# Graph kernel on one core: columns of h and of scores laid out by partition group

## Chip, cores and metric

The kernel runs on one core of a Trainium2 chip. The metric is device time in microseconds for one execution of the whole program, as a median of several runs. Smaller is better.

## What is computed

x holds 64 graphs of 256 nodes with 512 features each, in float32; adj is one 256 x 256 adjacency matrix of zeros and ones, shared by all graphs. Two residual layers follow each other:

```python
# layer 0
h = maximum(layernorm(x), 0)
q, k, v = h @ Wq.T, h @ Wk.T, h @ Wv.T
rel = adj.T * (q @ k.T)                     # per graph, 256 x 256
rel = rel / norm(rel, axis=-1)
x = x + rel @ v
# layer 1
h = maximum(layernorm(x), 0)
x = x + (adj @ h) @ weight + bias
```

## The kernel before

**Precision.** Each float32 operand of a large product is split into three parts of fewer bits, with the suffixes u, l and s. A product is three passes of matmuls; before the third, ScalarE scales the bank in place (L340). So one product of 512 x 512 by 512 rows costs 12 matmuls of 512 columns, and each operand needs one pass of ScalarE and two of VectorE for its parts (L238 to L249, L316 to L318, L471 to L473).

**Tiling.** The graphs are taken in 32 pairs of two (512 rows, as four chunks of 128 rows on the partitions). M = Wq.T Wk is formed once. For each pair there are six stages: g (`g_stage`, gy = M times h transposed, from m_u, m_l, m_s and h_u, h_l, hs), v (`v_stage`), the scores (`scores`), the weighted sum (`attend`), layer 1's sum over neighbours (`gather`) and its product with weight (`mix`). `gather` and `mix` of a pair run during the next pair. A pair begins on TensorE with the first matmul bank<-h_u,m_u, and that is how pairs are told apart here; they are numbered from 0.

**Order.** `Plan` takes operations with an engine, a cost, keys that they read and write, a time to landing and, for some, a number of microseconds by which they should be early. `order` gives each a due time, counted back from an ideal TensorE, and then simulates the engines to choose an order. That order is written out by hand to each engine: every engine runs strictly in it. An instruction that waits holds all that stand behind it on its engine.

**Two transposes by way of VectorE.** Products need h, and later the scores, with features or neighbours on the partitions. VectorE transposes 32 x 32 blocks only (`V.transpose`). So the 16 combinations of four partition groups of 32 and four column groups of 32 are first exchanged: 16 DMAs within SBUF carry the block (k, j) to partition group j, column group k.

- h: the relus (L279, one for each of the four chunks) write h_rel, which is `[chunk c, 512 features]`; `h_place` (L293) copies it into blocks, and `h_turn` (L301) transposes blocks into ht. `h_parts` splits ht into h_u (L316, ScalarE), h_l (L318) and hs (L308). In h_rel the 32 columns of one group are 128 bytes, so each DMA takes 512 pieces of 128 bytes.
- scores: `scores` multiplies the bank with adj transposed and writes rel, which is the first half of h_rel (L415, VectorE), and squares it for the norm (L419, ScalarE). `turn_scores` copies rel into placed, the second half of h_rel, by 16 DMAs of 256 pieces of 128 bytes (L455), and transposes placed into raw (L461), from which rel_u, rel_l and rel_s_parts come (L471, L472, L473). For pairs 0, 1 and 31, TensorE transposes the scores instead (L437).

h_rel thus serves twice in a pair: the scores of pair i, then h of pair i + 1.

**SP's queue.** SP issues, in its fixed order, the 16 placements of h of the next pair, the load of x for the pair after that into fresh (L257), the load of x for the running pair into x_ring, and the 16 placements of scores. The statistics of fresh (L265, L266 on VectorE) wait for that load. Stores of finished pairs go out from POOL's queue (L564).

Of the kernel before, what the change touches and what calls it, by code (L numbers as in the profile page):

```python
# [12 lines left out]
AF = mybir.ActivationFunctionType  # L13
# [95 lines left out]
def f(ap):  # L109
    return ap.bitcast(F32)  # L110
# [3 lines left out]
def kernel(  # L114
# [11 lines left out]
    nc = tc.nc  # L126
    P = 128
    B, N, D = x.shape
    DC = D // P
    NC = N // P  # L130
    NB = 2
    TC = NB * NC
    T = NB * N
    NP = B // NB
    S = 32
# [18 lines left out]
    ht, h_s = [None, None], [None, None]  # L154
# [5 lines left out]
    blocks = room("blocks", TC, DC, P)  # L160
    h_rel = room("h_rel", TC, D)
    bias_bc = room("bias_bc", D)
    wv_sb, w_sb = blocks.rearrange("p c d n -> p c (d n)"), ring[1]
    ident = room("ident", P)
# [16 lines left out]
    def raw():  # L181
        return changing("rel_s", "raw", NB, D)

    def rel_third():
        return changing("rel_s", "parts", NB, NC, NC, P, dtype=F32R)

    flat_rel = h_rel.rearrange("p c d -> p (c d)")
    rel = flat_rel[:, : T * NC].rearrange("p (b k m) -> p b k m", b=NB, k=NC)
    placed = flat_rel[:, T * NC :].rearrange("p (b k t n) -> p b k t n", b=NB, k=NC, t=NC)

    stats = [
        [
# [15 lines left out]
    V, A, G, SP = nc.vector, nc.scalar, nc.gpsimd, nc.sync  # L208
# [10 lines left out]
        (in_pieces.add if turned else in_pieces.discard)(n)  # L219
        return bank[n], ("bank", n)  # L220

    placed_all = [("blocks", j, k) for j in range(P // S) for k in range(P // S)]

    def keys(name, n=DC):
        return [(name, k) for k in range(n)]
# [56 lines left out]
    def h_rows(plan, i, src=fresh, name="fresh"):  # L282
        relu, needs = norm(plan, i, 0, src, name)
        for c in range(TC):
            plan.add("ACT", 0.72, lambda c=c: relu(h_rel[:, c, :], c),
                     [(name, c), *needs], [("h_rel", c)])

    def h_place(plan, early=8.0):
        hv = h_rel.rearrange("p c (d e) -> p c d e", e=P)

        for j in range(P // S):
            for k in range(P // S):
                plan.add("SP", 0.65, lambda j=j, k=k: SP.dma_start(  # L293
                    out=blocks[ts(j, S), :, :, ts(k, S)], in_=hv[ts(k, S), :, :, ts(j, S)]),
                    keys("h_rel", TC), [("blocks", j, k)], lands=2.3, early=early)

    def h_turn(plan):
        def turn(k):
            ht[k] = room(f"ht{k}", 2, T, tag=f"h_s{k}")
            for d in range(2):  # L300
                V.transpose(ht[k][:, d].rearrange("p (c n) -> p c n", c=TC), blocks[:, :, 2 * k + d])  # L301
        for k in range(2):
            plan.add("DVE", 1.16, lambda k=k: turn(k), placed_all, [("h_s", 2 * k), ("h_s", 2 * k + 1)])

# [99 lines left out]
    def scores(plan, i):  # L404
        rn = norms[i % 2]
        for b in range(NB):
            def outs_of(ps, k, d, b=b):
                return [
                    (ps[:, ts(n, N)], gy[k][:, d, ts(b * NC + n, P)], hp(k, d)[:, ts(b, N)])
                    for n in range(NC)  # L410
                ]
            first, second = three(None, None, gy_half(b), h_named, 2 * HALF, outs_of)

            def drain(ps, key, b=b):
                plan.add("DVE", 0.6, lambda: V.tensor_mul(  # L415
                    rel[:, b].rearrange("p k m -> p (k m)"), ps, f(adjt[0]).rearrange("p k m -> p (k m)")),
                    [key, "adjt"], [("h_rel", b)])
                for k in range(NC):
                    plan.add("ACT", 0.53, lambda k=k: A.activation(  # L419
                        ps[:, ts(k, N)], rel[:, b, k], AF.Square, accum_out=rn[:, b, k : k + 1]),  # L420
                        [("h_rel", b)], [key, (f"rn{i % 2}", b, k)])
            unit(plan, first, second, drain)

    def turn_scores(plan, i, by_pe=False):
        rn, name = norms[i % 2], f"rn{i % 2}"
        sums = [(name, b, k) for b in range(NB) for k in range(NC)]
        plan.add("ACT", 0.2, lambda: A.activation(rn, rn, AF.Sqrt), [], sums)
        plan.add("DVE", 0.12, lambda: V.reciprocal(rn, rn), [], sums)
        if by_pe:
            u, l = (part.rearrange("p b t k n -> p b (t k n)") for part in rel_p)  # L430
            for b in range(NB):
                ps, key = next_bank(turned=True)

                def go(ps=ps, b=b):
                    for t in range(NC):
                        for k in range(NC):
                            nc.tensor.transpose(ps[:, ts(t * NC + k, P)], rel[:, b, k, ts(t, P)], ident)  # L437

                def third(b=b):
                    V.scalar_tensor_tensor(rel_third()[:, b].rearrange("p t k n -> p (t k n)"),  # L440
                                           f(l[:, b]), CROSS, f(u[:, b]), op0=ALU.mult, op1=ALU.subtract)
                plan.add("PE", 0.44, go, [("h_rel", b)], [key])
                plan.add("ACT", 0.49, lambda ps=ps, b=b: A.activation(
                    u[:, b], ps, AF.Copy, scale=NEAR), [key], [("rel_u", b)])
                plan.add("DVE", 0.63, lambda ps=ps, b=b: V.tensor_sub(
                    l[:, b], ps, f(u[:, b])), [key, ("rel_u", b)], [("rel_l", b)])
                plan.add("DVE", 0.6, third, [("rel_u", b), ("rel_l", b)],
                         [("raw", 0), ("raw", 1)] if not b else [("raw", 1)])
            return
        rv = rel.rearrange("p b k (t m) -> p (b k t) m", m=P)  # L450
        pv = placed.rearrange("p b k t n -> p (b k t) n")

        for j in range(P // S):
            for k in range(P // S):
                plan.add("SP", 0.65, lambda j=j, k=k: SP.dma_start(  # L455
                    out=pv[ts(j, S), :, ts(k, S)], in_=rv[ts(k, S), :, ts(j, S)]),
                    [("h_rel", 0), ("h_rel", 1)], [("placed", j, k)], lands=2.1)
        halves, rel_u, rel_l = ([(name, b) for b in range(NB)] for name in ("raw", "rel_u", "rel_l"))
        for b in range(NB):
            for k in range(NC):  # L460
                plan.add("DVE", 0.33, lambda b=b, k=k: V.transpose(  # L461
                    raw()[:, b].rearrange("p (t k n) -> p t k n", t=NC, k=NC)[:, :, k], placed[:, b, k]),
                    [("placed", j, t) for j in range(P // S) for t in range(P // S)] + [("h_rel", 2), ("h_rel", 3)], halves if not b and not k else halves[b : b + 1])

        def whole(ap):
            return ap.rearrange("p b t k n -> p (b t k n)")

        def flat_raw():
            return raw().rearrange("p b d -> p (b d)")
        u, l = (whole(part) for part in rel_p)  # L470
        plan.add("ACT", 0.96, lambda: A.activation(u, flat_raw(), AF.Copy, scale=NEAR), halves, rel_u)  # L471
        plan.add("DVE", 1.14, lambda: V.tensor_sub(l, flat_raw(), f(u)), [*halves, *rel_u], rel_l)  # L472
        plan.add("DVE", 1.14, lambda: V.scalar_tensor_tensor(  # L473
            whole(rel_third()), f(l), CROSS, f(u), op0=ALU.mult, op1=ALU.subtract), [*rel_u, *rel_l], halves)
# [204 lines left out]
    def pairs(exact):  # L679
# [15 lines left out]
        v_stage(plan, 0, exact, (0, 1))  # L695
        scores(plan, 0)
        v_stage(plan, 0, exact, (2, 3))
        turn_scores(plan, 0, by_pe=True)
        finish(plan)
        h_turn(plan)  # L700
        h_parts(plan)
# [3 lines left out]
        for i in range(1, NP):  # L705
            last = i + 1 == NP
            load(plan, i, name=f"x{i % 2}")
            if not last:
                h_rows(plan, i + 1)
                h_place(plan)  # L710
            if i + 2 < NP:
                load(plan, i + 2)
            g_stage(plan, i)
            v_stage(plan, i, exact, (0,))
            v_stage(plan, i, exact, (1,), hold=True)
            scores(plan, i)
            gather(plan, i - 1, exact)
            while held:
                held.pop(0)()
            if last or i == 1:  # L720
                turn_scores(plan, i, by_pe=True)
            v_stage(plan, i, exact, (2, 3))
            if not last:
                if i > 1:
                    turn_scores(plan, i)
                waiting.append(lambda: (h_turn(plan), h_parts(plan)))
                mix(plan, i - 1)
            attend(plan, i, exact)
            if last:
                mix(plan, i - 1)  # L730
                gather(plan, i, exact)
            store(plan, i - 1)
# [37 lines left out]
```

## Time and profile before

| | before |
|---|---|
| runs | 1570.98, 1572.20, 1574.19 us; median 1572.2 |
| profiled execution | 1571.74 us, span 1570.0 us |
| instructions in the profile | 22385 |
| placements of h | 496 DMAs of 64 KB, 2.1 us from issue to landing |
| placements of scores | 464 DMAs of 32 KB, 1.9 us |
| loads into fresh | 31 DMAs of 1 MB, 5.9 us |
| loads into x_ring | 31 DMAs of 1 MB, 7.9 us |
| transposes of h, L301 | 124 of 128x512, 688 ns each |
| transposes of scores, L461 | 116 of 128x256, 404 ns each |
| products with adj, L415 | 64 of 128x512, 691 ns each |
| relus into h_rel, L279 | 124 of 128x512, 808 ns each |
| squares, L419 | 128 of 128x256, 391 ns each |

The profile records one execution; its own time is beside its span. Engine names are PE (TensorE matmul), PEld (its weight loads), DVE (VectorE), ACT (ScalarE), POOL, and SPq for SP's issues of DMAs. Matmuls overlap, and their ends are modelled, so the length of a matmul in the profile is more than the distance from one to the next; where PE loses time is seen in the distance of starts. A wait is written as waiter <- releaser. Times in windows are counted from the start of the span.

### The profile page before, as it was taken

Reading aid. Unit: us, or ns where it says so; the run is one execution under the profiler, and the core shown is the slowest. Engines: PE = TensorE matmul, PEld = TensorE weight load, DVE = VectorE, ACT = ScalarE, POOL = GpSimd, SP = SyncE. Lnnn points to the kernel's source line nnn. Section 1 sums busy time; section 2 is a strip of 40 time slices with the busy share of each in tenths; the row PEclk is TensorE's granted clock in tenths of the full one; section 3 lists DMA queues with packets and bytes.
Section 4 is the critical chain, followed back from the end, with each engine's and each line's share of the span. In section 5 each row is a group of like instructions: output and inputs, shape, how many; then the busy total and the mean of one; then the engine's idle time right before and its main releaser. Section 6 shows DMA issues by size and latency. Waiting matters only on the chain.

```text
span 1570.0 us, 22385 instructions
## 1 busy us (share of the span) xinstructions
PE 1557.2 (99%) x8046; PEld 1322.8 (84%) x8046; DVE 1357.6 (86%) x2419; ACT 1023.8 (65%) x1941; POOL 24.3 (2%) x39
## 2 busy tenths in 40 slices
PE   9999999999999999999999999999999999999998
PEld 6788888888888888888888888888888888888886
DVE  6997889898888988898888889888989888988786
ACT  5567666676667676666666676766666766767654
POOL 0000000000000000000000000000000000000000
PEclk9999999999999999999999999999999999999999
DMA  6431444324444334443244442344433344433311
GB/s 195 113 81 41 118 111 120 69 77 111 115 115 93 82 81 120 110 119 68 77 112 114 114 112 67 81 118 111 118 75 85 97 119 110 121 67 79 84 54 56
DMA packets 433127, 153.62 MB, mean 98 GB/s; under 512 B 389872, under 2 KB 390128, under 8 KB 433008
## 3 DMA queue, kind: packets, MB, share of 16 engines
q1 hardware_dynamic: 422784, 116.46, 31.5%
q0 software_dynamic: 8432, 32.51, 5.6%
q10 hardware_dynamic: 1792, 3.15, 0.5%
q8 instruction: 65, 1.06, 0.3%
q14 instruction: 54, 0.44, 0.1%
HBM read 70.78 MB, written 33.55 MB: 66 GB/s over the span
## 4 chain that ended last, share of the span: by engine, by line
PE 83%; SPq 5%; DVE 5%; DMA 4%; ACT 2%; issue 1%; ACTq 0%; DVEq 0%
PE bank L228 83%; SPq L293 4%; DMA fresh<-in_x_dram 2%; SPq L455 2%; ACT h_rel L279 1%; DVE st L265 1%; DMA bias_bc<-in_L_gnn_bias_dram 1%; DMA x_ring<-in_x_dram 1%; DMA h_rel<-h_rel 0%; DVE gy_s L239 0%; DVE gy_l L241 0%; ACT bank L340 0%; DVE h_rel L415 0%; DVE late_parts L239 0%; DVE mv L266 0%
## 5 line engine op out<-in xcount | busy, mean ns | idle before, releaser
L340 ACT ACTIVATE bank<-bank 128x512 f32<-128x512 f32 x572 | 333.4, 583 | 321.5 <-PE bank L228 318.3
L228 PE MATMUL bank<-wv_s,hs 128*128 128x512 f32 x512 | 139.9, 395 | 0.2
L228 PE MATMUL bank<-w_u,gy_u 128*128 128x512 f32 x512 | 137.9, 391 | 0.0
L228 PE MATMUL bank<-wv_u,h_u 128*128 128x512 f32 x512 | 137.6, 390 | 0.0
L228 PE MATMUL bank<-w_s,gy_s 128*128 128x512 f32 x512 | 137.5, 391 | 0.0
L228 PE MATMUL bank<-w_l,gy_l 128*128 128x512 f32 x512 | 137.3, 390 | 0.0
L228 PE MATMUL bank<-wv_l,h_l 128*128 128x512 f32 x512 | 136.9, 389 | 0.0
L228 PE MATMUL bank<-h_u,m_u 128*128 128x512 f32 x512 | 136.5, 389 | 0.3 <-DVE m_s L239 0.3
L228 PE MATMUL bank<-h_l,m_l 128*128 128x512 f32 x512 | 136.6, 389 | 0.1
L228 PE MATMUL bank<-hs,m_s 128*128 128x512 f32 x512 | 136.3, 389 | 0.0
L239 DVE SCALAR_TENSOR_TENSOR gy_s<-gy_u,bank 128x512 fp32r<-128x512 f32 x128 | 86.2, 676 | 43.3 <-ACT gy_u L238 43.3
L228 PEld LDWEIGHTS bank<-w_u,gy_u 128*128 128x128 f32 x512 | 96.0, 188 | 20.8
L228 PEld LDWEIGHTS bank<-w_s,gy_s 128*128 128x128 f32 x512 | 95.7, 188 | 21.2 <-ACT bank L340 1.2
L228 PEld LDWEIGHTS bank<-w_l,gy_l 128*128 128x128 f32 x512 | 96.1, 188 | 20.7
L228 PEld LDWEIGHTS bank<-h_u,m_u 128*128 128x128 f32 x512 | 96.0, 188 | 20.5 <-ACT wv_u L238 0.5
L228 PEld LDWEIGHTS bank<-h_l,m_l 128*128 128x128 f32 x512 | 96.0, 188 | 20.4 <-DVE h_l L318 0.5
L228 PEld LDWEIGHTS bank<-wv_l,h_l 128*128 128x128 f32 x512 | 96.1, 188 | 20.2
L228 PEld LDWEIGHTS bank<-hs,m_s 128*128 128x128 f32 x512 | 96.1, 188 | 19.9
L228 PE MATMUL bank<-adjt_r,late_parts 128*128 128x256 f32 x896 | 112.8, 277 | 0.0
L228 PEld LDWEIGHTS bank<-wv_s,hs 128*128 128x128 f32 x512 | 92.8, 188 | 22.8 <-ACT bank L340 5.2
L228 PEld LDWEIGHTS bank<-wv_u,h_u 128*128 128x128 f32 x512 | 93.7, 188 | 17.8
L228 PEld LDWEIGHTS bank<-adjt_r,late_parts 128*128 128x128 f32 x896 | 107.5, 188 | 0.0
(110 smaller groups left out, 3078.3 us busy)
## 6 DMA issues: line engine op xcount, KB each, us to landing
fresh<-in_x_dram SPq DMA_DIRECT2D x31, 1024.0 KB, 5.9
blocks<-h_rel SPq DMA_DIRECT2D x496, 64.0 KB, 2.1
x_ring<-in_x_dram SPq DMA_DIRECT2D x31, 1024.0 KB, 7.9
out_dram<-x_ring POOLq DMA_DIRECT2D x31, 1024.0 KB, 5.3
h_rel<-h_rel SPq DMA_DIRECT2D x464, 32.0 KB, 1.9
blocks<-in_L_gnn_Wv_dram ACTq DMA_DIRECT2D x1, 1024.0 KB, 10.9
x_ring<-in_L_gnn_weight_dram SPq DMA_DIRECT2D x1, 1024.0 KB, 12.4
out_dram<-x_ring SPq DMA_DIRECT2D x4, 256.0 KB, 2.3
```

The lines of the kernel that those rows point to most:

```text
L228: nc.tensor.matmul(out, left, right, start=first, stop=True, skip_group_check=True)
L239: plan.add("DVE", 0.63, lambda: V.scalar_tensor_tensor(s(), f(u()), ONE, ps, op0=ALU.mult, op1=ALU.subtract), [*key, *ku], ks)
L265: V.bn_stats(st[:, c, :], src[:, c, :])
L279: A.activation(dst, src[:, c, :], AF.Relu, bias=nb[:, c : c + 1], scale=rs[:, c : c + 1])
L293: plan.add("SP", 0.65, lambda j=j, k=k: SP.dma_start(out=blocks[ts(j, S), :, :, ts(k, S)], in_=hv[ts(k, S), :, :, ts(j, S)]), keys("h_rel" ...
L340: plan.add("ACT", 0.49, lambda: A.activation(ps, ps, AF.Copy, scale=ONE), [], [key])
L455: plan.add("SP", 0.65, lambda j=j, k=k: SP.dma_start(out=pv[ts(j, S), :, ts(k, S)], in_=rv[ts(k, S), :, ts(j, S)]), [("h_rel", 0), ("h_rel ...
```

## The change

h_rel, blocks, rel and placed keep their size and place in memory, but the order of columns within them changes. Until now the columns of h_rel were (chunk, feature block d, column group j, 32 columns); now the column group j is outermost: (j, chunk, d, 32 columns). The scores get the same treatment, (j, b, k, t, 32 columns). The columns that one placement moves then lie together in each partition: 2 KB for h, 1 KB for scores. `place` issues the 16 DMAs for both; each moves 32 pieces.

The operands of the engines follow: relus write, and transposes read, runs of 32 floats; so do the products with adj and the squares where the scores are placed by DMA. Pairs that TensorE transposes keep the plain order of scores (`plain`, `by_pe`), and so does h of pair 0. Since a relu of one chunk now touches all four column groups, the first relu of a pair claims all four parts of h_rel, and the other three depend on it.

```diff
+    J = P // S
     flat_rel = h_rel.rearrange("p c d -> p (c d)")
-    rel = flat_rel[:, : T * NC].rearrange("p (b k m) -> p b k m", b=NB, k=NC)
-    placed = flat_rel[:, T * NC :].rearrange("p (b k t n) -> p b k t n", b=NB, k=NC, t=NC)
+    flat_score, flat_placed = flat_rel[:, : T * NC], flat_rel[:, T * NC :]
+    rel, placed = (part.rearrange("p (j b k t s) -> p b k t j s", j=J, b=NB, k=NC, t=NC)
+                   for part in (flat_score, flat_placed))
+    plain = flat_score.rearrange("p (b k m) -> p b k m", b=NB, k=NC)
+    def by_pe(i):
+        return i < 2 or i + 1 == NP
+    flat_blocks = blocks.rearrange("p c d n -> p (c d n)")
+    h_cols, h_placed = (part.rearrange("p (j c d s) -> p c d j s", j=J, c=TC, d=DC)
+                        for part in (flat_rel, flat_blocks))
+    def place(plan, src, dst, keys_in, name, lands, early=0.0):
+        width = src.shape[1] // J
+        for j in range(J):
+            for k in range(J):
+                plan.add("SP", 0.65, lambda j=j, k=k: SP.dma_start(
+                    out=dst[ts(j, S), ts(k, width)], in_=src[ts(k, S), ts(j, width)]),
+                    keys_in, [(name, j, k)], lands=lands, early=early)
...
     def h_rows(plan, i, src=fresh, name="fresh"):
         relu, needs = norm(plan, i, 0, src, name)
         for c in range(TC):
-            plan.add("ACT", 0.72, lambda c=c: relu(h_rel[:, c, :], c),
-                     [(name, c), *needs], [("h_rel", c)])
+            plan.add("ACT", 0.72, lambda c=c: relu(h_rel[:, c, :] if name == "x0" else h_cols[:, c], c),
+                     [(name, c), *needs, *([("h_rel", 0)] if c else [])], [("h_rel", c)] if c else keys("h_rel", TC))
     def h_place(plan, early=8.0):
-        hv = h_rel.rearrange("p c (d e) -> p c d e", e=P)
-        for j in range(P // S):
-            for k in range(P // S):
-                plan.add("SP", 0.65, lambda j=j, k=k: SP.dma_start(
-                    out=blocks[ts(j, S), :, :, ts(k, S)], in_=hv[ts(k, S), :, :, ts(j, S)]),
-                    keys("h_rel", TC), [("blocks", j, k)], lands=2.3, early=early)
+        place(plan, flat_rel, flat_blocks, keys("h_rel", TC), "blocks", 2.3, early)
     def h_turn(plan):
...
-                V.transpose(ht[k][:, d].rearrange("p (c n) -> p c n", c=TC), blocks[:, :, 2 * k + d])
+                V.transpose(ht[k][:, d].rearrange("p (c k s) -> p c k s", c=TC, k=J), h_placed[:, :, 2 * k + d])
...
             def drain(ps, key, b=b):
+                dst = plain[:, b].rearrange("p k (t j s) -> p k t j s", t=NC, j=J) if by_pe(i) else rel[:, b]
+                def columns(part):
+                    return part.rearrange("p (k t j s) -> p k t j s", k=NC, t=NC, j=J)
                 plan.add("DVE", 0.6, lambda: V.tensor_mul(
-                    rel[:, b].rearrange("p k m -> p (k m)"), ps, f(adjt[0]).rearrange("p k m -> p (k m)")),
+                    *(part.rearrange("p k t j s -> p (k t) j s") for part in (
+                        dst, columns(ps), columns(f(adjt[0]).rearrange("p k m -> p (k m)")))),),
                     [key, "adjt"], [("h_rel", b)])
                 for k in range(NC):
                     plan.add("ACT", 0.53, lambda k=k: A.activation(
-                        ps[:, ts(k, N)], rel[:, b, k], AF.Square, accum_out=rn[:, b, k : k + 1]),
+                        columns(ps)[:, k], dst[:, k], AF.Square, accum_out=rn[:, b, k : k + 1]),
                         [("h_rel", b)], [key, (f"rn{i % 2}", b, k)])
...
-        for j in range(P // S):
-            for k in range(P // S):
-                plan.add("SP", 0.65, lambda j=j, k=k: SP.dma_start(
-                    out=pv[ts(j, S), :, ts(k, S)], in_=rv[ts(k, S), :, ts(j, S)]),
-                    [("h_rel", 0), ("h_rel", 1)], [("placed", j, k)], lands=2.1)
+        place(plan, flat_score, flat_placed, [("h_rel", 0), ("h_rel", 1)], "placed", 2.1)
...
                 plan.add("DVE", 0.33, lambda b=b, k=k: V.transpose(
-                    raw()[:, b].rearrange("p (t k n) -> p t k n", t=NC, k=NC)[:, :, k], placed[:, b, k]),
-                    [("placed", j, t) for j in range(P // S) for t in range(P // S)] + [("h_rel", 2), ("h_rel", 3)], halves if not b and not k else halves[b : b + 1])
+                    raw()[:, b].rearrange("p (t k j s) -> p t k j s", t=NC, k=NC, j=J)[:, :, k], placed[:, b, k]),
+                    [*(("placed", j, k) for j in range(J) for k in range(J)), ("h_rel", 2), ("h_rel", 3)],
+                    halves if not b and not k else halves[b : b + 1])
```

More of the change, by code (lines that the diff above doesn't have):

```diff
@@ L220, in next_bank @@
         return bank[n], ("bank", n)
-    placed_all = [("blocks", j, k) for j in range(P // S) for k in range(P // S)]
+    placed_all = [("blocks", j, k) for j in range(J) for k in range(J)]
     def keys(name, n=DC):
@@ L419, in drain, with turn_scores @@
                     plan.add("ACT", 0.53, lambda k=k: A.activation(
-                        ps[:, ts(k, N)], rel[:, b, k], AF.Square, accum_out=rn[:, b, k : k + 1]),
+                        columns(ps)[:, k], dst[:, k], AF.Square, accum_out=rn[:, b, k : k + 1]),
                         [("h_rel", b)], [key, (f"rn{i % 2}", b, k)])
             unit(plan, first, second, drain)
-    def turn_scores(plan, i, by_pe=False):
+    def turn_scores(plan, i):
         rn, name = norms[i % 2], f"rn{i % 2}"
@@ L428, in turn_scores @@
         plan.add("DVE", 0.12, lambda: V.reciprocal(rn, rn), [], sums)
-        if by_pe:
+        if by_pe(i):
             u, l = (part.rearrange("p b t k n -> p b (t k n)") for part in rel_p)
@@ L436, in go @@
                         for k in range(NC):
-                            nc.tensor.transpose(ps[:, ts(t * NC + k, P)], rel[:, b, k, ts(t, P)], ident)
+                            nc.tensor.transpose(ps[:, ts(t * NC + k, P)], plain[:, b, k, ts(t, P)], ident)
                 def third(b=b):
@@ L449, in turn_scores @@
             return
-        rv = rel.rearrange("p b k (t m) -> p (b k t) m", m=P)
-        pv = placed.rearrange("p b k t n -> p (b k t) n")
-        for j in range(P // S):
-            for k in range(P // S):
-                plan.add("SP", 0.65, lambda j=j, k=k: SP.dma_start(
-                    out=pv[ts(j, S), :, ts(k, S)], in_=rv[ts(k, S), :, ts(j, S)]),
-                    [("h_rel", 0), ("h_rel", 1)], [("placed", j, k)], lands=2.1)
+        place(plan, flat_score, flat_placed, [("h_rel", 0), ("h_rel", 1)], "placed", 2.1)
         halves, rel_u, rel_l = ([(name, b) for b in range(NB)] for name in ("raw", "rel_u", "rel_l"))
@@ L697, in pairs @@
         v_stage(plan, 0, exact, (2, 3))
-        turn_scores(plan, 0, by_pe=True)
+        turn_scores(plan, 0)
         finish(plan)
@@ L719, in pairs @@
                 held.pop(0)()
-            if last or i == 1:
-                turn_scores(plan, i, by_pe=True)
+            if by_pe(i):
+                turn_scores(plan, i)
             v_stage(plan, i, exact, (2, 3))
             if not last:
-                if i > 1:
+                if not by_pe(i):
                     turn_scores(plan, i)
```

## The prediction

> **What bounds the kernel now.** I read the page's busy times first, then the waits, then the start of every pair in the timeline of TensorE (PE), and last the timelines of SP and VectorE (DVE) in pairs that lose time and pairs that don't. The page's first two parts:
>
> ```profile
> PE 1557.2 (99%) x8046; PEld 1322.8 (84%) x8046; DVE 1357.6 (86%) x2419; ACT 1023.8 (65%) x1941; POOL 24.3 (2%) x39
> ...
> PEclk9999999999999999999999999999999999999999
> ...
> DMA packets 433127, 153.62 MB, mean 98 GB/s; under 512 B 389872, under 2 KB 390128, under 8 KB 433008
> ```
>
> PE is busy all the time and at full clock, and the change takes no matmul away. So all that can be won is the time in which PE waits; and since matmul ends are modelled, I look for it in start times. The first matmul on h_u and m_u opens a pair. Four such starts, from PE's timeline (start, length, engine, line):
>
> ```profile
> 113.45 1.07 PE L228 MATMUL bank<-h_u,m_u 128*128 128x512 f32 x4
> ...
> 257.28 1.07 PE L228 MATMUL bank<-h_u,m_u 128*128 128x512 f32 x4
> ...
> 304.82 1.07 PE L228 MATMUL bank<-h_u,m_u 128*128 128x512 f32 x4
> ...
> 1499.06 1.07 PE L228 MATMUL bank<-h_u,m_u 128*128 128x512 f32 x4
> ```
>
> The pair that starts at 257.28 takes 47.54 us. So do 12 other pairs, to 0.01 us: this is the floor, matmul behind matmul. From 113.45 to 1499.06 are 29 pairs (numbers 2 to 30), 1385.61 us; at the floor they would be 29 x 47.54 = 1378.66 us. Their whole loss is 6.95 us. What makes it? The view of waits (waiter <- releaser: us in total, times, longest):
>
> ```profile
> DVE st L265 <- DMA fresh<-in_x_dram: 13.8, 19, 1.4
> ACT h_rel L279 <- DMA h_rel<-h_rel: 12.0, 18, 1.6
> DVE rel_s_raw L461 <- DMA h_rel<-h_rel: 1.0, 2, 0.7
> ```
>
> The worst pair starts at 783.58 and takes 48.61 us. SP's, DVE's and PE's timelines in it:
>
> ```profile
> 779.17 13.45 SPq L293 DMA_DIRECT2D blocks<-h_rel  x16
> 792.67 0.62 SPq L257 DMA_DIRECT2D fresh<-in_x_dram  x1
> 793.39 0.44 SPq L257 DMA_DIRECT2D x_ring<-in_x_dram  x1
> ...
> 798.54 0.69 DVE L265 BATCH_NORM_STATS2 st<-fresh 128x6 f32<-128x512 f32 x1 [0.72 <-DMA fresh<-in_x_dram]
> ...
> 800.85 0.69 DVE L241 SCALAR_TENSOR_TENSOR gy_l<-gy_s,gy_u 128x512 fp32r<-128x512 f32 x1
> ...
> 801.60 0.50 PE L228 MATMUL bank<-h_l,gy_l 128*128 128x256 f32 x2 [0.34 <-DVE gy_l L241]
> ```
>
> SP needs 13.45 us to issue the 16 placements of h, and only then can it issue the load of fresh. The load lands 5.9 us later, DVE stands at the statistics with gy_s and gy_l queued behind them, and PE waits for gy_l. Set against the pair's start, these statistics begin at 14.96. In the clean pair from 257.28 (DVE's and SP's timelines) they begin at 13.29, without a wait:
>
> ```profile
> 264.40 0.62 SPq L257 DMA_DIRECT2D fresh<-in_x_dram  x1
> ...
> 270.57 0.69 DVE L265 BATCH_NORM_STATS2 st<-fresh 128x6 f32<-128x512 f32 x1
> ```
>
> I set all 29 pairs side by side in this way. The ten whose statistics begin at 14.2 or later lose 0.27 to 1.07 us each; of those at 14.1 or earlier only two lose more than 0.1, and these (from 113.45 and 1118.2; 0.33 and 0.51 us), with 0.07 in the pair from 1070.6, lose it at about 42, where the score transposes (L461) began late, at 37.4 to 37.8 and not at 36.9. In the steady part every loss of weight hangs on SP's two series of small transfers.
>
> **What the Trainium skill says.** "DMA: Bandwidth & Descriptors", section "Queues, rings and completion order": each DMA engine takes turns between queues, packet by packet. A 128-byte piece can then stand behind a 4 KB packet of the store at each turn. The trace fits: placements land in 2.0 to 2.1 us, but in up to 5.1 us in the worst pair, where a store runs beside them. The same page, "Specifications", wants at least 512 bytes for full rate. In the stretch 425.4 to 432.4, where only score placements run, the share is 0.26 of 16 engines for 11 x 256 pieces: 0.26 x 16 x 7.0 / 2816 = some 10 ns for 128 bytes. "SBUF — State Buffer", section "Specifications (TRN2)", row on cachelines: an access that hits each 16-byte line at least twice keeps full bandwidth, so a run of 32 floats should cost nothing; no operation here has runs that short. "Vector Engine (DVE) Microarchitecture Reference", section "3. Layer 2 — the DVE datapath", gives the transpose one element per cycle per lane; 688 ns for 512 elements, against 684 for an ordinary two-input operation, agrees.
>
> **The change, part by part.**
>
> *The placements.* 16 for h in 30 pairs, 16 for scores in 29, each now 32 pieces of 2 KB or 1 KB. DMA time falls, but PE doesn't wait for that; what counts is SP. An issue of many pieces takes 0.63 us (h) or 0.61 (scores), and some of h take 1.4 or more. A plain issue isn't in the trace between SBUF partitions. From below: 0.33, the load of wq_last by itself. From above: 0.65, as now. I take 0.44, the load of x_ring right behind another issue, plus 0.02 between: 16 x 0.46 = 7.4 us, against 12.2 (the clean pair) to 13.45. I also expect the long issues to go, as each DMA engine gets two pieces per transfer, not 32.
>
> *The relus.* A relu of one chunk now writes into all four column groups, so all four wait until the score transposes are done. In the built order the first one, until now between the two h_u copies (at 388.88 in ACT's timeline), comes behind the third. The last relu then ends 0.7 us later (one relu's pitch), and so does the first placement. ACT has 35% free there, and behind it the copies of banks (L340) wait 0.8 to 1.2 us for PE anyway: no cost. The wait for score placements (12.0 us over 18 times) is covered by the earlier rel_u.
>
> *Sum for fresh.* +0.7 for the relus, -4.8 to -6.0 for the issues: issued 4.1 to 5.3 us earlier. The worst pair needs 1.7 (14.96 - 13.29). Even at 0.65 per issue without long ones it is 13.45 - 10.5 - 0.7 = 2.2 us. So statistics stop waiting in all pairs. Late next is nothing up to the floor: PE itself.
>
> *Scores.* Last issue now at 34.8 after the pair's start, landing 1.9 later, 36.7, with the transposes at 36.9: almost no room. At 0.46 per issue they land about 3 us earlier. Together with fresh: the 6.95 us go, all of them; I book 6.9.
>
> *DVE and ACT operands.* Per pair four transposes of h (688 ns), four of scores (404), two products (691), four relus (808) and four squares (391) get runs of 32 floats. From below zero, as the element counts are the same. From above I have only a rival's price, below. I take 0.
>
> *Start-up.* Two things move in the built order. DVE stood 3.46 us at h_l (L636, from 18.2 to 21.65) with the last two statistics behind it (1.6 us); they now come before it, into that hole. m_s at 25.99 starts earlier by what ACT's copies allow; PE waits for it (0.31). Bounds 0 and 1.6, I take 0.4. In pair 1 (from 63.7, 49.75 us) two relus, 1.5 us, stand before the squares on ACT; gy_u and then DVE's L248 (1.00 idle) and L239 are late, and PE waits 0.69 us for L239. They move behind. Bounds 0 and 0.7, I take 0.5.
>
> *Moved and free.* PE's and SP's order is the same as before. The PE transposes of pairs 0, 1 and 31 keep their layout. Stalls of the last pair (1.3 us near 1534) don't touch placements and stay.
>
> Sum: 6.9 + 0.4 + 0.5 = 7.8. The profiled execution took 1571.74 (span 1570.0 and 1.74 around it), 0.5 below the median of the runs, 1572.2: 1571.74 - 7.8 = 1563.9, and I forecast 1564.0.
>
> **Rivals.**
> *A, slower: runs of 32 floats cost DVE time in the transposes.* Eight lie in a row before rel_u, with a busy sum of 4 x 0.688 + 4 x 0.404 = 4.4 us. Pairs with transposes 0.5 us late lose 0.07 and 0.9 us late 0.5: 0.4 us is free, the rest goes straight to PE. With L us more, 29 x (L - 0.4) is lost; from L = 0.7, transposes 16% longer, this eats the 7.8 and decides. At 25% (L = 1.1): 1563.9 + 20 = 1584. At double length it would be near 1680. For it: nothing measured here has such runs. Against: the cacheline rule, and reads in four runs of 128 already take only 688.
> *B, no change worth naming: SP is no faster.* If an issue between partitions stays near 0.63 and the long ones stay too, the 0.7 us of the relus come on top, and fresh is as late as now. What's left is scores and start-up: 0.3 to 3 us, some 1570.5. For it: fresh (0.62) has large pieces too, and takes as long as a placement. Against: by itself a load takes 0.33 to 0.38.
> *C, the change doesn't do what it says* (pieces stay small because the copies are cut again): as B.
>
> **How the numbers follow.** Main case 0.70: 1562 to 1567.5, depending on how much of start-up and of the 6.9 comes. B with C 0.16: 1568 to 1572.5. A 0.14: above 1574. Below 1561.5 almost nothing is left to win, as PE's floor stands there. The range 1561.5 to 1572 leaves A and little else outside, under 2 in 10. 0.2% (3.1 us) is what a measurement can tell from no change: faster 0.70 + 0.03 of B, same 0.13, slower 0.14.
>
> **What would show it.** Right: pairs 2 to 30 at 47.54 almost throughout, no wait of statistics for fresh, 16 placements in some 7 us on SP, packets under 512 B near 17,000 (389872 less 496 x 512 and 464 x 256), the transposes at 688 and 404 ns. Wrong: transposes above 0.75 us, placements at 0.6 us each, or a new wait before the scores' products; then A or B is to be read there.

## The result, and the profile after

The changed kernel takes 1564.82 us (median of six runs, 1564.42 to 1565.35), against 1572.2 before: a ratio of 0.9952 with a 95% interval of 0.9942 to 0.9962, some 7.4 us less. The profiled execution of it took 1564.82 us itself. The forecast was 1564.0, with a range of 1561.5 to 1572.0.

From the page of the kernel after, first the busy times, then packets, then its DMA queue q1 (packets, MB, share of 16 engines), then the chain of waits by engine:

```profile
span 1563.0 us, 22543 instructions
...
PE 1550.2 (99%) x8046; PEld 1322.6 (85%) x8046; DVE 1355.9 (87%) x2419; ACT 1022.5 (65%) x1941; POOL 24.4 (2%) x39
...
DMA packets 91112, 153.63 MB, mean 98 GB/s; under 512 B 17136, under 2 KB 32240, under 8 KB 90992
...
q1 hardware_dynamic: 80768, 116.46, 24.7%
...
PE 95%; DVE 3%; DMA 0%; ACT 0%; issue 0%; DVEq 0%
```

The same chain before:

```profile
PE 83%; SPq 5%; DVE 5%; DMA 4%; ACT 2%; issue 1%; ACTq 0%; DVEq 0%
```

The small packets went exactly as the layout says: 17136 under 512 bytes are left of 389872. Queue q1 was 31.5% busy before; 0.315 x 1570.0 - 0.247 x 1563.0 = some 108 us are gone on each of the 16 DMA engines. That is far more than the 7.4 us won, so most of it was never waited for; what part of it counts through a faster landing of fresh is looked at below. What counts is that the chain is now 95% PE, where it was 83%, with 5% on SP's issues and 4% on DMA.

TensorE's timeline after, at the start of pairs 2, 29, 30 and 31 (start, length, engine, line):

```profile
112.96 0.84 PE L248 MATMUL bank<-h_u,m_u 128*128 128x512 f32 x3
...
1396.71 0.84 PE L248 MATMUL bank<-h_u,m_u 128*128 128x512 f32 x3
...
1444.63 0.62 PE L248 MATMUL bank<-h_u,m_u 128*128 128x512 f32 x2
...
1492.17 0.62 PE L248 MATMUL bank<-h_u,m_u 128*128 128x512 f32 x2
```

Pairs 2 to 30 take 1492.17 - 112.96 = 1379.21 us, against 1385.61 before. At the floor of 47.54 they would take 1378.66, so 0.55 us of loss is left of 6.95. The worst pair is 29, with 47.92. The view of waits after says the same (waiter <- releaser: us in total, times, longest):

```profile
DVE st L285 <- DMA fresh<-in_x_dram: 4.9, 7, 2.4
```

It was 13.8 us in 19 waits. One of the seven, 2.42 us long, is in the start-up at 16.73. ScalarE's wait for landing scores (12.0 us in 18 waits) is gone from the list. So the time came from where the forecast looked for it, the late load of fresh.

The way from there to PE is only in part the one that the forecast named, gy_l. The weight loads of TensorE whose wait shrank most are those of hs in the v stage, which wait until ScalarE has scaled a bank. Their groups on the pages before and after (busy us, mean ns of one | idle before, releaser):

```profile
L228 PEld LDWEIGHTS bank<-wv_s,hs 128*128 128x128 f32 x512 | 92.8, 188 | 22.8 <-ACT bank L340 5.2
...
L248 PEld LDWEIGHTS bank<-wv_s,hs 128*128 128x128 f32 x512 | 93.8, 188 | 19.3 <-ACT bank L354 0.9
```

Set against a clean pair, the starts of PE's matmuls in the kernel before slip at two places: some 17 to 28 us after a pair's start, where gy_l and what follows it is used, mainly in the pairs with the latest statistics, and at about 30 us, at this weight load, in every pair that loses 0.1 us or more to late statistics. I estimate from these starts that the second place makes some 3 of the 6.95 us. In the pair from 497.05, which loses 0.28 us, it is the only one. These waits go and come with the late load in the experiments below: there are none with fresh first in the kernel after, and 9.5 us in 26 waits with two more transfers.

But SP's timeline after, for the pair that starts at 778.5, doesn't look as forecast:

```profile
774.10 12.34 SPq L207 DMA_DIRECT2D blocks<-h_rel  x16
786.49 0.58 SPq L277 DMA_DIRECT2D fresh<-in_x_dram  x1
```

Sixteen placements still take 12.34 us there, and not some 7. Single issues of that series, from the same timeline:

```profile
774.10 0.51 SPq L207 DMA_DIRECT2D blocks<-h_rel  x1
...
782.03 0.98 SPq L207 DMA_DIRECT2D blocks<-h_rel  x1
```

The first takes 0.51 us, most of those behind it 0.59, and some still take far more. Over all 496 placements of h the median issue is 0.589 us, where it was 0.628. Those longer than 0.7 us fell only from 81 to 68, and most of both stand at places 10 to 12 of a series. A series takes 11.62 us on average, where it took 12.70. The load itself is a little quicker too. From the page after (KB each, median us from issue to landing; it was 5.9):

```profile
fresh<-in_x_dram SPq DMA_DIRECT2D x31, 1024.0 KB, 5.7
```

The question for the experiments was therefore why 1.1 us less on SP was enough.

The pair that still loses most shows how close the edge is, the latest moment at which fresh can come without loss. SP and VectorE in pair 29 (start 1396.71), from the timeline after:

```profile
1392.26 13.03 SPq L207 DMA_DIRECT2D blocks<-h_rel  x16
1405.34 0.59 SPq L277 DMA_DIRECT2D fresh<-in_x_dram  x1
...
1410.94 0.69 DVE L285 BATCH_NORM_STATS2 st<-fresh 128x6 f32<-128x512 f32 x1 [0.86 <-DMA fresh<-in_x_dram]
```

Here the series was long again (13.03), fresh was issued 8.63 us after the pair's start, the statistics began at 14.23, and the pair lost 0.38 us. In the other 26 of the pairs 3 to 29, fresh is issued at 6.9 to 8.2.

### The profile page after: what moved, and what is told of

Same layout as the page of the kernel before. It is cut to its first block, busy times and chain, and to the rows that moved or that the text cites. A ratio compares the mean times of both kernels' runs of the same rounds, so it can differ in the third digit from the quotient of the medians.

```text
span 1563.0 us, 22543 instructions
## 1 busy us (share of the span) xinstructions
PE 1550.2 (99%) x8046; PEld 1322.6 (85%) x8046; DVE 1355.9 (87%) x2419; ACT 1022.5 (65%) x1941; POOL 24.4 (2%) x39
## 2 busy tenths in 40 slices
DMA packets 91112, 153.63 MB, mean 98 GB/s; under 512 B 17136, under 2 KB 32240, under 8 KB 90992
## 3 DMA queue, kind: packets, MB, share of 16 engines
q1 hardware_dynamic: 80768, 116.46, 24.7%
## 4 chain that ended last, share of the span: by engine, by line
PE 95%; DVE 3%; DMA 0%; ACT 0%; issue 0%; DVEq 0%
PE bank L248 95%; DMA fresh<-in_x_dram 0%; DVE late_parts L259 0%; DVE late_parts L261 0%; DVE rel_s_parts L459 0%; DVE st L285 0%; DVE gy_l L268 0%; DVE rel_l L464 0%; DVE wv_l L261 0%; DVE m_l L261 0%; DVE ht L315 0%; DVE wv_s L259 0%; DVE m_s L259 0%; DVE w_l L261 0%; DVE h_l L332 0%
```

## The experiments

The theory: SP's 16 placements push the load of fresh to an edge, and every pair behind it loses. The placements got a little cheaper, and with that most loads come before the edge. The rivals: the gain comes from the relus' new key rule, from the placements of scores, or from the smaller load on the DMA engines.

**The relus' rule alone (before, nothing else changed).** The pieces stay at 128 bytes.

```diff
-                     [(name, c), *needs], [("h_rel", c)])
+                     [(name, c), *needs, *([("h_rel", 0)] if c else [])], [("h_rel", c)] if c else keys("h_rel", TC))
```

> The kernel before, with nothing but the changed rule for the relus: the first relu of a pair claims all of h_rel, so ScalarE and VectorE run in the order of the changed kernel, while all pieces stay at 128 bytes. Theory 'fresh comes late because of SP's series': the placements start 0.7 us later and are as long as before (12.7 us on average), so fresh comes later still; the gain of pair 1 (some 0.7 us) stays, the loss of pairs 2 to 30 grows: 1572 to 1580 us, statistics waiting for fresh in 20 pairs or more. Theory 'the order of the relus did it, since ScalarE no longer stops at the first relu for the landing of scores': 1564.5 to 1566 us, pairs at 47.54.

Measured: 1578.69 us (1577.23 to 1579.59), ratio 1.0042, interval 1.0029 to 1.0056. The later relus, which the new layout forces, cost 6.2 us by themselves, against the 1572.48 that the kernel before took beside this run and the next three. The timeline of that run, in the pair that starts at 448.7 and takes 49.02 us:

```profile
444.30 13.78 SPq L293 DMA_DIRECT2D blocks<-h_rel  x16
458.12 0.62 SPq L257 DMA_DIRECT2D fresh<-in_x_dram  x1
...
464.11 0.69 DVE L265 BATCH_NORM_STATS2 st<-fresh 128x6 f32<-128x512 f32 x1 [2.00 <-DMA fresh<-in_x_dram]
...
467.17 0.50 PE L228 MATMUL bank<-h_l,gy_l 128*128 128x256 f32 x2 [0.75 <-DVE gy_l L241]
```

This is the chain of the kernel before, made longer: fresh issued 9.4 us after the pair's start, the statistics 2.00 us late, PE idle for gy_l. The waits of the statistics rise to

```profile
DVE st L265 <- DMA fresh<-in_x_dram: 25.8, 27, 2.3
```

So the gain isn't the relus' rule; the pieces had to win back its 6.2 us and 7 more.

**Only h in the new layout (after, with scores laid out as before).**

```diff
-    rel, placed = (part.rearrange("p (j b k t s) -> p b k t j s", j=J, b=NB, k=NC, t=NC)
+    rel, placed = (part.rearrange("p (b k t j s) -> p b k t j s", j=J, b=NB, k=NC, t=NC)
...
-        place(plan, flat_score, flat_placed, [("h_rel", 0), ("h_rel", 1)], "placed", 2.1)
+        rv, pv = (part.rearrange("p (q m) -> p q m", m=P) for part in (flat_score, flat_placed))
...
+                    out=pv[ts(j, S), :, ts(k, S)], in_=rv[ts(k, S), :, ts(j, S)]),
...
```

> The changed kernel with the scores back in their old layout (256 pieces of 128 bytes), h in pieces of 2 KB. Theory 'fresh': the series for h is what stands ahead of the load, so nearly all of the gain stays: 1564.5 to 1566.5 us. Theory 'scores': if the shorter series of scores carried it, most of the gain goes: 1569 to 1572 us.

Measured: 1564.40 us (1563.86 to 1564.78), ratio 0.9952, interval 0.9939 to 0.9966: the whole gain. Against the run before it, in which ScalarE, VectorE and SP work in the same order, 2 KB pieces for h are worth 1578.69 - 1564.40 = 14.3 us. Transposes of scores wait for their placements 2.8 us in five waits there; the pair from 1110.79 loses 0.24 us by it, the others next to nothing.

**Only scores in the new layout (h and the relus as before).**

```diff
-    h_cols, h_placed = (part.rearrange("p (j c d s) -> p c d j s", j=J, c=TC, d=DC)
+    h_cols, h_placed = (part.rearrange("p (c d j s) -> p c d j s", j=J, c=TC, d=DC)
...
-                     [(name, c), *needs, *([("h_rel", 0)] if c else [])], [("h_rel", c)] if c else keys("h_rel", TC))
+                     [(name, c), *needs], [("h_rel", c)])
...
```

The placements of h take pieces of 32 columns again.

> The kernel before with only the scores in the new layout (pieces of 1 KB), h in 128-byte pieces and with the old rule for the relus. Theory 'fresh': the series for h is as long as before, but the scores land some 0.5 us earlier, so the first relu waits less and the series starts a little earlier: a part of the gain, 1567 to 1571.5 us. Theory 'scores carried it': 1565 to 1566 us. If scores don't matter: 1572 us.

Measured: 1571.54 us, ratio 0.9995, interval 0.9987 to 1.0004: no effect that can be told from none. This half of the change does nothing for the time that could be measured.

**Fresh first (before, with the load of fresh issued on SP ahead of the 16 placements of h).** Nothing of the layout is changed; the DMA engines move the same small packets.

```diff
...
+            if fn in self.loads:
+                while out and at and out[at - 1] not in self.relus and out[at - 1] not in self.loads:
+                    at -= 1
+                first = [n for n in range(at, len(out)) if out[n] in self.places]
+                at = first[0] if first else len(out)
+            out.insert(at, fn)
...
```

> The kernel before with one edit in the order of SP's queue: in each pair the load of fresh goes out ahead of the 16 placements of h, instead of behind them. Layout, pieces and the order on all other engines stay. Theory 'fresh': no statistics wait, pairs 2 to 30 stand at 47.54 us, so 6 to 6.9 us are won without any change of pieces: 1565.5 to 1566.5 us. Rival 'the size of pieces or the order of the relus itself': 1570 to 1572 us.

Measured: 1566.39 us (1565.93 to 1567.60), ratio 0.9965, interval 0.9953 to 0.9978. SP's timeline, in the pair that starts at 779.34:

```profile
774.89 0.37 SPq L269 DMA_DIRECT2D fresh<-in_x_dram  x1
775.37 14.43 SPq L305 DMA_DIRECT2D blocks<-h_rel  x16
```

The placements take longer than ever, 14.43 us (14.22 on average), and land 3.4 us after issue instead of 2.1. PE doesn't care: pairs 2 to 30 lose 1.28 us in all. The waits of this run that touch these tiles:

```profile
ACT h_rel L291 <- DMA h_rel<-h_rel: 13.5, 19, 1.6
...
DVE st L277 <- DMA fresh<-in_x_dram: 0.6, 1, 0.6
```

The first is as large as before (12.0); of the second one wait is left, in the start-up. So ScalarE's wait for scores costs at most the 1.28 us; the statistics' wait was the loss. It goes although the DMA engines carry the same small packets as before, so a smaller load on them isn't needed for the gain. This doesn't show that it has no part in the gain of the new layout. Pair 1 still takes 49.76 us, and 49.77 with only the scores changed, but 49.29 with the relus' rule alone: most of its gain belongs to that rule.

**The same move in the kernel after.**

> The changed kernel with the load of fresh ahead of the 16 placements of h on SP, all else as it is. Theory 'fresh': the load has some 9 us more room, the last stalls of pairs 2 to 30 (0.6 us in sum) go and nothing else can: 1563.5 to 1565 us, the same as the changed kernel within the measurement. If large loads ahead of the placements hurt them: placements land later, h's transposes wait, above 1566 us.

Measured: 1565.91 us (1565.55 to 1566.09), ratio 0.9959, interval 0.9946 to 0.9973. The expectation was missed: every pair from 2 to 30 runs at the floor (0.07 us of loss in all), and still the time isn't below that of the kernel after. The end differs. The last addition on VectorE and the span, from the page and VectorE's timeline of this run:

```profile
span 1564.1 us, 22598 instructions
...
1555.98 0.69 DVE L580 TENSOR_TENSOR x_ring<-bank,x_ring 128x512 f32<-128x512 f32 x1 [0.27 <-PE bank L260]
```

From the end of that addition to the end of the span are 7.4 us. In the kernel after they are 5.1 (its last addition starts at 1557.24), and in the other runs 5.1 to 5.5; 5.2 in the run before this one, which issues its loads just as early. The trace shows where most of the difference lies: the last store lands 2.8 us after the addition in both, and then, among the waits that close the program, SP stands from 3.9 to 5.8 us after the addition, where in the kernel after it goes on at once. So no work of the kernel is late. The run below asks once more whether the move is at fault.

**Fresh ahead of the last four placements only (after).** Against the run above, one line differs:

```diff
-                at = first[0] if first else len(out)
+                at = first[-4] if first else len(out)
```

> After, but the load of fresh is issued on SP behind the first twelve placements of h and ahead of the last four. In the run with fresh ahead of all sixteen, every pair from 2 on ran at 47.54 us, and yet the program ended 5 us or more after its last addition, some 2.3 us later than in the other runs. If those 2.3 us come from the loads standing ahead of the whole series (theory: the order on SP costs something at the end), half of this should stay or go in step with the move. If they are an accident of that one program, the end goes back to about 5.1 us after the last addition, all pairs stay at 47.54 us, no wait of the statistics is left, and the time is 1563.3 to 1564.4. Rival: the four placements that now land behind a 1 MB load come late, their transposes wait, and pairs lose again: 1565 or more.

Measured: 1563.96 us (1563.35 to 1564.01), ratio 0.9950, interval 0.9936 to 0.9963. All pairs 2 to 30 at the floor (0.02 us lost), and 5.1 us from the last addition to the end. So neither of the two other programs with the load moved pays the 2.3 us. What makes SP stand there stays open; one program alone shows it. This is the fastest version, but its interval lies on that of the kernel after: the two can't be told apart.

**Two more, and four more, transfers between the placements and fresh (after).** Each moves 32 pieces of 448 bytes into room that nothing else uses, so that SP has more to issue. The transposes of h are made to wait for them as well, but neither trace has a wait on them.

```diff
+        for j in range(2):
+            plan.add("SP", 0.0, lambda j=j: SP.dma_start(
+                out=level[ts(j, S)], in_=flat_rel[ts(j, S), :112]),
+                keys("h_rel", TC), [("level", j)], lands=2.3, early=early)
...
```

> The changed kernel with two more DMAs (32 pieces of 448 bytes into room that nothing reads) behind the 16 placements of h and ahead of the load of fresh. Order on the other engines stays. Theory 'fresh': the load goes out 1.2 to 1.3 us later; some 0.6 us after 7.3 are free, the rest is lost in each of 27 pairs: 15 us or so, 1572 to 1584 us. Rival 'the gain came from pieces as such, or from DMA time': two small DMAs more change nothing, 1564 to 1566 us.

> The same with four more DMAs. Theory 'fresh': 2.5 us later, of which 0.6 are free: 1.9 us x 27 pairs, some 50 us: 1600 to 1625 us, and the statistics wait in all pairs. Rival 'pieces as such': 1564 to 1567 us.

Measured: with two 1575.82 us (ratio 1.0026, interval 1.0017 to 1.0035), with four 1614.15 (1.0267, interval 1.0253 to 1.0281). The timeline with four, in the pair that starts at 1399.24 and takes 49.73 us:

```profile
1394.80 12.05 SPq L207 DMA_DIRECT2D blocks<-h_rel  x16
1406.90 2.49 SPq L311 DMA_DIRECT2D level<-h_rel  x4
1409.43 0.58 SPq L277 DMA_DIRECT2D fresh<-in_x_dram  x1
...
1414.92 0.69 DVE L285 BATCH_NORM_STATS2 st<-fresh 128x6 f32<-128x512 f32 x1 [2.31 <-DMA fresh<-in_x_dram]
...
1417.98 0.50 PE L248 MATMUL bank<-h_l,gy_l 128*128 128x256 f32 x2 [1.05 <-DVE gy_l L261]
```

Four issues take 2.49 us, fresh is issued 10.2 us after the pair's start, VectorE stands for 2.31 us with gy_s and gy_l behind it, and PE for 1.05. The waits of that run:

```profile
DVE st L285 <- DMA fresh<-in_x_dram: 63.0, 29, 3.3
```

Two issues put the kernel back behind where it began, and two more cost 1614.15 - 1575.82 = 38.3 us, or 1.3 us in each of 29 pairs for 1.25 us of issues. Behind the edge the loss goes nearly one to one with SP's time.

**Short stores (after, the stores of pairs 2 to 29 cut to 16 of their 512 columns).** The other 496 columns of these results are not written.

```diff
-        plan.add("POOL", 0.8, lambda: G.dma_start(out=outs[i], in_=ring[slot]),
+        plan.add("POOL", 0.8, lambda: G.dma_start(out=outs[i][:, :, :16] if 1 < i < NP - 2 else outs[i],
+                                                  in_=ring[slot][:, :, :16] if 1 < i < NP - 2 else ring[slot]),
```

> The changed kernel with the stores of pairs 2 to 29 cut to 16 of 512 columns, so those pairs' results are not in the output. It asks what makes some issues of placements take 1 us or more, at the 10th to 12th of 16. Theory 'a store that runs beside them': these long issues go, a series of 16 takes 10.0 to 10.3 us throughout, fresh goes out 1.4 us earlier. Rival 'something of SP itself': the series stays at 11.5 us in the median. The time is 1563.5 to 1565 us in both cases, since fresh has just enough room already.

One execution: 1564.60 us. SP's timeline at the same place as the kernel after above:

```profile
774.10 10.23 SPq L207 DMA_DIRECT2D blocks<-h_rel  x16
784.38 1.75 SPq L277 DMA_DIRECT2D fresh<-in_x_dram  x1
```

A series takes 10.43 us on average instead of 11.62, and of the 68 long issues 16 are left. So most long issues come with the store of the pair before: POOL issues it 4.8 us after the start of a series, and it is under way when places 10 to 12 are issued. What makes the other 16 (the 1.75 us of fresh here is a long one too) wasn't tried.

All runs in one table. The loss is the time of pairs 2 to 30 above 29 x 47.54; the mean issue and the mean landing of fresh are counted from the start of its pair, over pairs 3 to 29. All are those of the profiled executions; that of four more took 1618.71 us, 4.6 above its median, and that of two more 1574.43, 1.4 below.

| | mean issue of fresh, us | mean landing, us | pairs with statistics after 13.9 us | loss, us |
|---|---|---|---|---|
| fresh first, after | -4.43 | 1.81 | 0 | 0.07 |
| fresh first, before | -4.95 | 0.98 | 1 | 1.28 |
| before the last four | 4.67 | 11.91 | 0 | 0.02 |
| short stores | 6.04 | 11.74 | 1 | 0.28 |
| after | 7.34 | 13.07 | 2 | 0.55 |
| only h | 7.42 | 13.19 | 6 | 0.53 |
| before | 7.91 | 13.85 | 13 | 6.94 |
| only scores | 7.92 | 13.96 | 14 | 7.35 |
| relus' rule alone | 8.36 | 14.32 | 19 | 14.10 |
| two more | 8.60 | 14.18 | 22 | 10.41 |
| four more | 9.99 | 15.58 | 27 | 52.95 |

Up to a mean of some 7.4 us next to nothing is lost to the statistics, at 7.9 it is 7 us, and from there it climbs steeply. The relus' rule alone loses more than two extra transfers, though its load goes out 0.24 us earlier. The landing settles it: it comes 0.14 us later there, since that load takes longer. What counts is when fresh arrives, and pair by pair it comes out plainly. Of the 297 pairs 3 to 29 of these runs, 105 have statistics that begin after 13.9 us, and 98 of them lose, to within 0.15 us, just the time by which they begin after 13.9. The largest exceptions are four pairs with four more transfers, beyond 16.4 us, which lose over a microsecond more.

This also puts a size on the third rival. From before to after fresh arrives 0.78 us earlier on the mean: 0.57 by its issue, and 0.21 because it lands faster (5.95 and 5.74 us on the mean). In the three runs with 128-byte pieces of h and the load behind the placements it takes 5.95 to 6.04 us, in the five with 2 KB pieces 5.58 to 5.77. So the smaller load on the DMA engines probably has a share, the lesser one; no run changes it alone.

## Why the prediction was right, step by step

**Where the loss was.** Right. Pairs 2 to 30 lost 6.95 us, and 6.40 of them are gone (1385.61 - 1379.21). That the late load of fresh was the cause is shown by the fresh-first run, which moves that one instruction in the kernel before and takes the loss from 6.94 to 1.28 us, and by the extra transfers, which bring it back. Of the way to PE, the prediction had the half by gy_l; the other, by a bank that ScalarE scales at about 30 us in a pair, it didn't name.

**The price of an issue.** Wrong, and this is the mis-sized term. The prediction put 0.44 us and 0.02 between, 7.4 us for 16, taken from the load of x_ring. Measured were 0.589, with a pitch of 0.63, and 11.62 us on average. It also had the long issues go; 68 of 81 stayed. The load of x_ring was the wrong neighbour: it comes from HBM and follows a load from HBM, though why such an issue is shorter isn't shown. The nearer sign was the upper bound that the prediction had named itself, 0.65. And "placements at 0.6 us each" was its own sign of being wrong, to be read as rival B: the sign came, rival B's time did not.

**The relus.** Right: where nothing else delays it, the last relu of a pair ends 0.7 us later (42.3 us after the pair's start for its beginning, 41.6 before). Some pairs before were already late by the wait for scores, so the series of placements starts 0.54 us later on the mean. The prediction did not see what this would cost alone, 6.2 us, if SP gained nothing.

**The sum for fresh.** 4.1 to 5.3 us earlier was forecast; it is 0.57 on the mean (7.91 to 7.34), near +0.54 for the start of the series and -1.13 for its length in these pairs. That the landing would be 0.21 us shorter was not in the sum. The 0.57 is even less than the 2.2 us that the prediction gave as the poor case, since that case let the long issues go.

**Why the time came out all the same.** The loss has an edge. The prediction had read it from the kernel before (pairs with statistics up to 14.1 us lose almost nothing) but used it only to ask whether 4 us were enough. The edge lies where the loads of the kernel before were spread, from 7.05 to 9.09 us; 13 pairs were beyond it, and 0.57 us, with the 0.21 of the landing, brought their number to two. Rival B had the premise right (issues near 0.63, long ones staying), and yet its conclusion, fresh as late as now, doesn't follow: the balance of +0.54 and -1.13 is small, but falls at the steep place. By this sum one more issue of 0.63 us in the series would have used up the 0.57; with two, the kernel was slower than before. So the time within 1 us of the measured one was in good part luck, and no sign of a good estimate of the step.

**Scores.** 3 us earlier was forecast; the series of issues fell from 10.70 to 10.17 us, 0.5. The small losses near 42 us in a pair, which the prediction put down to the scores, fit it: they stand in one to three pairs of each run that has the scores in 128-byte pieces (before, only h, fresh first before, the relus' rule alone), at most 0.4 us a pair, and in none with the new ones. In sum that is under 1.3 us in a run, and the run with only scores shows that it can't be told from nothing.

**Runs of 32 floats (rival A).** Right at zero. The groups after (busy us, mean ns of one | idle before):

```profile
L315 DVE STREAM_TRANSPOSE ht<-blocks 128x512 f32<-128x512 f32 x124 | 80.5, 688 | 7.7 <-PE bank L248 6.4 <-DMA h_rel<-h_rel 1.3
...
L473 DVE STREAM_TRANSPOSE rel_s_raw<-h_rel 128x256 f32<-128x256 f32 x116 | 40.2, 404 | 0.4 <-issue 0.3
```

688 and 404 ns, to the nanosecond what they were. The relus take 806 (808 before), the products 692 (691), the squares 391 (391). The rule on cachelines in the Trainium skill, "SBUF — State Buffer", section "Specifications (TRN2)", agrees with all five: a run of 32 floats fills 16-byte lines, so nothing is lost.

**Start-up and pair 1.** Pair 1 takes 49.08 us instead of 49.75, 0.67 against a forecast of 0.5. The start-up's 0.4 is there, but drowned: from the first h_l (L636) to m_s on VectorE are 4.34 us in the kernel before and in the two runs with its order, and 3.94 in the kernel after and the other seven. The first h_l itself, though, began anywhere from 21.54 to 22.32 us in these eleven runs, and in the profile after it was the latest of all. Pair 1 thus starts at 63.88, against 63.70.

**The sum.** In the two profiled executions: +0.2 to the start of pair 1, -0.7 in it, -6.4 in pairs 2 to 30, and under 0.1 from pair 31 on: 6.9 us of span, 1570.0 to 1563.0 as rounded. The forecast had 7.8.

**A reading that doesn't hold.** That placements land in up to 5.1 us in the worst pair does not set it apart: in the clean pair from 257.28 it is up to 5.5 us. And the 496 placements of h are 31 series, not the 30 that it counts; nothing in its sum rests on either.

## What to carry to other kernels

Where a loss comes from an instruction that is issued too late in a queue, first find the edge, the latest issue at which nothing is lost, and set it against the spread of the present issues: near the edge half a microsecond can be worth all or nothing, so a small term in the queue needs a measured price. Before pieces are enlarged to save a queue time, ask whether the one late instruction can go ahead of the series; here moving a single load gave 0.9965 of the time, against 0.9952 for the new layout. And a new layout brings its new dependences: here the relus' rule would have cost 6 us had the pieces not won 14.

## What the runs showed of the hardware

The time for which SP issues a transfer between SBUF partitions hardly depends on the number of its pieces: 0.628 us for 512 pieces of 128 bytes, 0.589 for 32 of 2 KB, 0.51 for the first of these after a pause. On the DMA engines the size of the pieces does count: q1's share fell from 31.5% to 24.7% for the same bytes. The Trainium skill, "DMA: Bandwidth & Descriptors", section "Why small descriptors are slow (HBM only)", says that transfers within SBUF don't suffer the penalty of small pieces; here part of such a penalty is measured.

Most long issues (over 0.7 us) come with the store beside them: there are 68 of 496 with full stores, 16 with short ones. A load of fresh just ahead of the series makes 136 with 128-byte pieces, where there were 81, but only 54 with 2 KB pieces. So a large transfer beside them is not by itself enough to make issues long; what does stays open.
